# Adjacency and basis products of a four-layer graph network, issued per batch as 64x64x64 quarters of TensorE instead of 128x128x128 block-diagonal products

## The chip, the cores and the metric

The kernel runs on one core of a Trainium2 chip. The metric is the device time of one launch in microseconds (us); three executions of the kernel before took 2379.05, 2380.96 and 2382.34 us, so the median is 2380.96 us. The engines are named as in the profile: PE is TensorE's matmul stream and PEld its weight loads, DVE is VectorE, ACT is ScalarE, POOL is GpSimd and SP the queue of SyncE that issues DMAs.

## What is computed

The input x holds 128 batches of 64 nodes with 256 features, in float32, and one 64x64 adjacency matrix `adj` serves all batches. Four layers follow one another, and each ends in `x = layernorm(x + layer(x))`:

```python
# layer 0: two graph convolutions, then LSTMs over windows of 1 to 4 nodes
h = relu(einsum('ts,bsh->bth', adj, x @ Wg0 + bg0))
h = relu(einsum('ts,bsh->bth', adj, h @ Wg1 + bg1))
for p in 1..4: the last node of each window of p nodes becomes an LSTM's last state
# layer 1: normalized adjacency, two maps with batch norm over all rows
agg = einsum('nm,bmd->bnd', A_hat, x);  h = relu(bn(agg @ W1.T + b1));  out = bn(h @ W2.T + b2)
# layer 2: attention over 512 edges, 4 heads
# layer 3: U = eigenvectors of the normalized Laplacian (64x64)
agg = einsum('mn,bnd->bmd', U.T, x);  h = relu(agg @ W1 + b1)
out = einsum('nm,bmd->bnd', U, h @ W2 + b2)
```

So `adj` (layer 0, twice), `A_hat` (layer 1) and `U` (layer 3, twice) are each a 64x64 matrix that is applied to the 64 nodes of every batch separately. These are the products that the change touches.

## The kernel before

X stays in SBUF for the whole program as 64 tiles of 128 rows and 256 features; one tile holds two batches, batch b in rows 64b to 64b+63. A group of four tiles (index q) is the unit of work of all the stages below.

**The matrices.** `bda`, `bdah`, `bdu` and `bdut` are 128x128 tiles with the 64x64 matrix twice on the diagonal and zeros elsewhere (`bdu` and `bdut` reuse the tiles of `bda` and `bdah` later on, which is why the profile names them so). One product of a tile's 128-feature half with such a matrix handles two batches at once, and half of what it multiplies is zeros. The result comes out transposed, features in the rows, which is what the next map wants as its moving operand. Each float32 matmul leaves two records in the trace, so counts of records are twice the counts of calls.

**Layer 0.** `convolve(g, H)` does a group of 16 tiles in four q. For each q it forms `axT` (line 1566, copied by ACT on line 1568), multiplies by wg0 (line 1574, DVE line 1575), then by wg1 (line 1584, DVE line 1586) and applies the adjacency again (line 1592) with a relu copy by ACT into H (line 1594). It is a generator that yields after every PSUM evacuation, 8 times for each q. The first group runs alone, beside the sorting of the edges (`sort_edges`). The other three run inside `windows(...)`, the LSTM (lines 1624 and 1628, gates on ACT line 1630): `paced` spreads their steps evenly over the LSTM's matmuls of p = 3 and 4. The convolution has two PSUM buffers of its own (`pp`, `bufs=2`), the LSTM four (`pq`). A computation of the eigenvectors of 64x64 size runs beside the LSTM on DVE, in small pieces that `pump` issues (its matmuls are on line 148, 64 rows of the array each).

**Layer 1.** A first loop over 16 q multiplies by `bdah` (line 1787), copies with ACT to `at` (line 1789), multiplies by w1 (line 1793, sixteen records of four output blocks), takes statistics with DVE (line 1794), and copies the result away with ACT (line 1795). In the first eight q, transposes of layer 0's last group follow (line 1661). PSUM has seven buffers here. The inner part reads:

```python
for k in range(2):
    ps = pp.tile([P, 512], F32, tag="ps", name="ps")
    for j in range(4):
        te.matmul(ps[:, j * P : (j + 1) * P], X[:, q * 4 + j, k * P : (k + 1) * P], bdah, start=True, stop=True)
    s.copy(at[:, k, :], ps)
for c in range(4):
    ...
```

**Layer 2** is not changed, but its `mixed` (line 2125) already issues 64x64x64 matmuls: for one batch (64 rows) the four heads alternate between the two column halves of the array; the second batch follows, in another PSUM bank.

**Layer 3** is a software pipeline over q with four stages: `basis` (line 2211, copied by ACT line 2213; POOL then adds a constant to X, line 2215), `first_map` (line 2221, DVE line 2224), `back` (line 2229, ACT line 2231) and `second_map` (line 2239, whose sum and norm are `Norm.add` and `flush`, lines 1234 to 1253). A call of `blocks` runs stage k on q-k in the order 0, 1, 2, 3. The last part of layer 2 (`values`: line 2125, then 2146) is interleaved with it, two steps for each block. Six PSUM buffers serve both.

The order on each engine is fixed when the program is built: each engine works through its list in order, and a wait at the head of the list holds up all behind it.

Of the kernel before, what the change touches and what calls it, by code (L numbers as in the profile page):

```python
# [7 lines left out]
F32 = mybir.dt.float32  # L8
# [6 lines left out]
N = 64  # L15
NB = 128
D = 256
P = 128
# [1241 lines left out]
def tile_adj_resnorm(ctx: ExitStack, tc: tile.TileContext, I: dict, out: bass.AP, layers: int = 4):  # L1260
# [65 lines left out]
    bdah = const.tile([P, P], F32, tag="bdah", name="bdah")  # L1326
    bdu, bdut = bda, bdah


    ek = ctx.enter_context(tc.tile_pool(name="ek", bufs=1))  # L1330
    et = ctx.enter_context(tc.tile_pool(name="et", bufs=1))
# [178 lines left out]
    with tc.tile_pool(name="lw", bufs=1) as lw, tc.tile_pool(  # L1510
# [48 lines left out]
        def convolve(g, H):  # L1559

            for q in range(TG // 4):
                axT = lc.tile([P, 2, 512], F32, tag="ay", name="axT")
                for k in range(2):
                    ps = pp.tile([P, 512], F32, tag="ps", name="ps")
                    for j in range(4):
                        te.matmul(ps[:, j * P : (j + 1) * P], X[:, g * TG + q * 4 + j, k * P : (k + 1) * P],
                                  bda, start=True, stop=True)
                    s.copy(axT[:, k, :], ps)
                    yield
                h1 = lc.tile([P, 2, 512], F32, tag="h1", name="h1")  # L1570
                for c in range(2):
                    ps = pp.tile([P, 512], F32, tag="ps", name="ps")
                    for k in range(2):
                        te.matmul(ps, wg0[:, k, c * P : (c + 1) * P], axT[:, k, :], start=(k == 0), stop=(k == 1))
                    v.tensor_tensor(
                        h1[:, c, :].rearrange("p (b n) -> p b n", n=N), ps.rearrange("p (b n) -> p b n", n=N),
                        negc[:, c, None, :].to_broadcast([P, 8, N]), ALU.max)
                    yield
                y2 = lc.tile([P, 4, D], F32, tag="ay", name="y2")
                for j in range(0, 4, 2):  # L1580
                    ps = pp.tile([P, 512], F32, tag="ps", name="ps")
                    for i in range(2):
                        for k in range(2):
                            te.matmul(ps[:, i * D : (i + 1) * D], h1[:, k, (j + i) * P : (j + i + 1) * P],
                                      wg1[:, k, :], start=(k == 0), stop=(k == 1))
                    v.tensor_tensor(y2[:, j : j + 2, :], ps.rearrange("p (i d) -> p i d", i=2),
                                    b2c[:, None, :].to_broadcast([P, 2, D]), ALU.add)
                    yield
                for c in range(2):
                    ps = pp.tile([P, 512], F32, tag="ps", name="ps")  # L1590
                    for j in range(4):
                        te.matmul(ps[:, j * P : (j + 1) * P], y2[:, j, c * P : (c + 1) * P], bda,
                                  start=True, stop=True)
                    s.activation(H[:, c].rearrange("p (m j) -> p j m", j=TG)[:, q * 4 : q * 4 + 4, :],
                                 ps.rearrange("p (j m) -> p j m", j=4), AF.Relu)
                    yield

        def windows(l0, H, p, w, side):

# [78 lines left out]
        with tc.tile_pool(name="gk", bufs=1) as gk:  # L1678
            sort = sort_edges(gk, pq, "pq")
            next(sort)  # L1680
            for k, _ in enumerate(convolve(0, H)):
                if k == 3:
                    second_bias(gk)
                if k == 7:
                    degrees()
                if k > 9:
                    next(sort, None)
            load_x(1)
            for _ in sort:
                pass  # L1690
        LOAD = {p: (TG * 2 * (N // p) / 512) * (6 + 16 * (p - 1)) for p in range(1, 5)}
        with tc.tile_pool(name="l0g", bufs=1) as l0:
            back = iter(())
            for g in range(NT // TG):


                side = paced(back, TG // 2, LOAD[1] + LOAD[2] - 4)
                for p in (1, 2):
                    windows(l0, H, p, weights(p), side)
                for _ in back:  # L1700
                    pass
                last, more = H, iter(())
                if g < NT // TG - 1:
                    if g < NT // TG - 2:
                        load_x(g + 2)
                    H = new_h(g + 1)
                    more = convolve(g + 1, H)
                side = paced(more, TG * 2, LOAD[3] + LOAD[4] - 4)
                for p in (3, 4):
                    windows(l0, last, p, weights(p), side)  # L1710
                for _ in more:
                    pass
                if g < NT // TG - 1:
                    back = residual(g, last, pr, "pr")
# [66 lines left out]
    for q in range(NQ):  # L1781
        nc.sync.dma_start(xd[q], xq(q))
        at = la.tile([P, 2, 512], F32, tag="at", name="at")
        for k in range(2):
            ps = pp.tile([P, 512], F32, tag="ps", name="ps")
            for j in range(4):
                te.matmul(ps[:, j * P : (j + 1) * P], X[:, q * 4 + j, k * P : (k + 1) * P], bdah,
                          start=True, stop=True)
            s.copy(at[:, k, :], ps)  # L1789
        for c in range(4):  # L1790
            ps = pp.tile([P, 512], F32, tag="ps", name="ps")
            for k in range(2):
                te.matmul(ps, w1[:, k, c * P : (c + 1) * P], at[:, k, :], start=(k == 0), stop=(k == 1))  # L1793
            v.bn_stats(st1[:, c, q, :], ps)
            s.copy(first(q, c), ps)
        next(back, None)
        if q < NQ - 1:
            pump(4.5 if q < 8 else 6.5 if q < NQ - 2 else 3)
# [108 lines left out]
    with ExitStack() as l2:  # L1907
# [291 lines left out]
        with tc.tile_pool(name="l3s", bufs=2) as s3, tc.tile_pool(name="l3p", bufs=6, space=PSUM) as p3:  # L2199
# [5 lines left out]

            def basis(q):
                ag[q] = s3.tile([P, 2, 512], F32, tag="ag", name="ag")
                for k in range(2):
                    ps = bank()
                    for j in range(4):  # L2210
                        te.matmul(ps[:, j * P : (j + 1) * P], X[:, q * 4 + j, k * P : (k + 1) * P], bdu,  # L2211
                                  start=True, stop=True)
                    s.copy(ag[q][:, k, :], ps)
                for j in range(4):
                    nc.gpsimd.tensor_tensor(X[:, q * 4 + j, :], X[:, q * 4 + j, :], cb, ALU.add)

# [7 lines left out]
                v.tensor_tensor(h[q], four(ps), nb1[:, None, :].to_broadcast([P, 4, P]), ALU.max)  # L2224

            def back(q):
                ps, a = bank(), h.pop(q)
                for j in range(4):
                    te.matmul(ps[:, j * P : (j + 1) * P], a[:, j, :], bdut, start=True, stop=True)  # L2229
                uh[q] = s3.tile([P, 4, P], F32, tag="uh", name="uh")  # L2230
                s.copy(uh[q], four(ps))

            def second_map(q):
                a = uh.pop(q)
# [12 lines left out]
            def blocks():  # L2247

                NQ = NT // 4
                for q in range(NQ + 3):  # L2250
                    for k, stage in enumerate((basis, first_map, back, second_map)):
                        if 0 <= q - k < NQ:
                            stage(q - k)
                    yield
# [70 lines left out]
```

## Time and profile before

| what | value |
|---|---|
| executions | 2379.05, 2380.96, 2382.34 us |
| median | 2380.96 us |
| span of the profiled execution (first to last instruction) | 2376.5 us |
| median less that span | 4.5 us |
| PE busy / DVE / ACT / POOL | 96% / 76% / 41% / 4% |
| granted PE clock, mean | 0.992 |

The profile gives the span of the profiled execution and no separate launch time for it; the executions around it lie 2.6 to 5.8 us above the span, which is what stands before the first and after the last instruction. A busy PE in the page means that some matmul is in flight; how densely they are issued is read from their starts.

The stages, by the records: layer 0 lasts until 1508 us (its first convolution until 69 us), the first loop of layer 1 from 1508 to 1658 us, its second loop and the scores of layer 2 until about 2086 us, the values of layer 2 from 2086 us on, with layer 3 from 2190 us to the end.

### The profile page before, as it was taken

The numbers are of one execution on the slowest core, as the hardware profiler recorded it, in microseconds if no ns is written. First come the engines' busy times: TensorE is split into PE (matmuls) and PEld (weight loads), VectorE is DVE, ScalarE is ACT, GpSimd is POOL, SyncE is SP. The second block draws the span as 40 slices with busy tenths as digits, with TensorE's granted clock in tenths as the row PEclk, the third lists the DMA queues.
The fourth block names the chain that finished last, engine by engine and source line by source line (L and its number), as shares of the span: only waits on it lengthen the run. The fifth ranks groups of instructions, "written<-read, shape, count | busy, mean of one in ns | idle before, by whom it ended". The sixth has DMA issues, their size and how long they took to land. (4 is left out here: it accounts for less than half of the span.)

```text
span 2376.5 us, 29696 instructions
## 1 busy us (share of the span) xinstructions
PE 2285.6 (96%) x9094; PEld 1228.5 (52%) x9094; DVE 1807.6 (76%) x8366; ACT 973.5 (41%) x1754; POOL 88.0 (4%) x134
## 2 busy tenths in 40 slices
PE   8999999999999999999999999999999999999897
PEld 6445654444565544664544654454434343345787
DVE  5666666677887888878888888788867886656587
ACT  2432222242333243333243322333427875557575
POOL 0000000000000000000000000000000000101431
PEclk9999999999999999999999999999999999999999
DMA  7000000000100010100000110011210010311532
GB/s 221 22 17 36 1 36 1 36 18 18 54 1 36 1 54 18 54 2 35 23 32 18 54 36 1 1 69 71 87 56 23 27 39 27 102 36 43 135 96 72
DMA packets 44661, 101.52 MB, mean 43 GB/s; under 512 B 5296, under 2 KB 23856, under 8 KB 43216
## 3 DMA queue, kind: packets, MB, share of 16 engines
q1 hardware_dynamic: 38656, 84.90, 10.4%
q0 software_dynamic: 3984, 14.40, 2.2%
q8 instruction: 72, 1.18, 0.2%
q14 instruction: 93, 0.76, 0.1%
q10 hardware_dynamic: 1856, 0.28, 0.1%
HBM read 67.97 MB, written 31.59 MB: 42 GB/s over the span
## 5 line engine op out<-in xcount | busy, mean ns | idle before, releaser
L1624 PE MATMUL pq<-H,wi 128*128 128x512 f32 (+1 forms) x2016 | 836.1, 548 | 6.3 <-DVE H L1653 4.0
L1630 ACT ACTIVATE gate<-pq,bl 128x512 f32<-128x512 f32 (+1 forms) x504 | 317.5, 634 | 802.8 <-PE pq L1628 657.8
L1624 PEld LDWEIGHTS pq<-H,wi 128*128 128x128 f32 x2016 | 372.7, 191 | 332.2 <-issue 256.3
L1628 PE MATMUL pq<-lh,wh 128*128 128x512 f32 (+1 forms) x1152 | 483.6, 536 | 15.5 <-DVE lh L1648 12.3
L1628 PEld LDWEIGHTS pq<-lh,wh 128*128 128x128 f32 x1152 | 213.4, 190 | 212.0 <-issue 128.2
L2027 DVE SCALAR_TENSOR_TENSOR xs<-xs 128x512 f32<-128x512 f32 x256 | 166.0, 683 | 57.0 <-ACT xs L2026 56.0
L2026 ACT COPY xs<-l 128x512 f32<-128x512 f32 x256 | 136.6, 585 | 73.8 <-PE l L2019 40.5
L1646 ACT ACTIVATE gate<-lc 128x512 f32<-128x512 f32 (+1 forms) x144 | 83.5, 580 | 165.6 <-DVE lc L1642 80.2
L2019 PE MATMUL l<-edge_s,xq 64*128 64x512 f32 x512 | 134.0, 616 | 9.5 <-ACT xs L2026 4.8
L1982 PE MATMUL m<-wqv,xT 128*128 128x512 f32 (+1 forms) x264 | 121.0, 596 | 0.9 <-DVE xT L1972 0.8
L1793 PE MATMUL ps<-at,w 128*128 128x512 f32 x256 | 115.0, 600 | 3.9 <-ACT at L1789 3.4
L1843 PE MATMUL ps<-h,w 128*128 128x512 f32 x256 | 112.3, 596 | 2.4 <-ACT h L1837 2.4
L1253 ACT ACTIVATE X<-X,ln_sh,ln_rs 128x256 f32<-128x256 f32 x192 | 99.9, 591 | 31.5 <-DVE ln_sh L1249 22.9
L1237 DVE BATCH_NORM_STATS2 ln_st<-X 128x6 f32<-128x256 f32 x256 | 98.6, 416 | 2.4
L142 DVE COPY AQR<-eps 64x192 f32<-64x192 f32 (+1 forms) x125 | 35.0, 280 | 83.5 <-PE eps L148 83.5
L1982 PEld LDWEIGHTS m<-wqv,xT 128*128 128x128 f32 x264 | 46.7, 189 | 73.9 <-issue 55.0
L1644 DVE TENSOR_TENSOR gate<-gate 128x512 f32<-128x512 f32 (+1 forms) x72 | 43.5, 605 | 47.4 <-ACT gate L1630 46.6
L1843 PEld LDWEIGHTS ps<-h,w 128*128 128x128 f32 x256 | 47.9, 190 | 60.6 <-issue 50.7
L2019 PEld LDWEIGHTS l<-edge_s,xq 64*128 64x128 f32 x512 | 46.1, 186 | 60.5 <-issue 31.7
L1793 PEld LDWEIGHTS ps<-at,w 128*128 128x128 f32 x256 | 46.6, 190 | 58.7 <-issue 46.0
L1653 DVE TENSOR_TENSOR H<-gate 128x512 f32<-128x512 f32 (+1 forms) x72 | 46.8, 650 | 35.0 <-ACT gate L1646 29.7
L129 DVE SCALAR_TENSOR_TENSOR CS<-GA,qE 64x1 f32<-64x1 f32 x294 | 61.7, 210 | 9.7
(586 smaller groups left out, 3231.5 us busy)
## 6 DMA issues: line engine op xcount, KB each, us to landing
wi<-in_WihT_dram SPq DMA_DIRECT2D x16, 1024.0 KB, 4.8
wh<-in_WhhT_dram SPq DMA_DIRECT2D x12, 1024.0 KB, 6.8
xd<-X SPq DMA_DIRECT2D x16, 512.0 KB, 2.8
X<-xd SPq DMA_DIRECT2D x16, 512.0 KB, 3.4
xv<-xv SPq DMA_DIRECT2D x32, 256.0 KB, 2.0
xr<-xv POOLq DMA_DIRECT2D x32, 256.0 KB, 2.9
X<-in_x_dram SPq DMA_DIRECT2D x15, 512.0 KB, 8.9
out_dram<-X SPq DMA_DIRECT2D x15, 512.0 KB, 2.9
```

Of the source, the lines that this page charges most:

```text
L1237: nc.vector.bn_stats(st, self.X[:, k, :])
L1253: nc.scalar.activation(x, x, AF.Identity, bias=sh[:, k : k + 1], scale=rs[:, k : k + 1])
L1624: te.matmul(ps, wi[:, kk, o * P : (o + 1) * P], at(kk, k), start=(kk == 0), stop=(k == 0 and kk == 1))
L1628: te.matmul(ps, wh[:, kk, o * P : (o + 1) * P], hst[:, kk, :M], start=False, stop=(kk == 1))
L1630: s.activation(gates[gt][:, c, :M], ps, AF.Tanh if gt == 2 else AF.Sigmoid, bias=bl[:, p - 1, o : o + 1])
L1646: s.activation(g[2], cs, AF.Tanh)
L1793: te.matmul(ps, w1[:, k, c * P : (c + 1) * P], at[:, k, :], start=(k == 0), stop=(k == 1))
L1843: te.matmul(ys[c], w2[:, k, c * P : (c + 1) * P], h[:, k, :], start=(k == 2), stop=(k == 1))
L1982: te.matmul(pss[i][:, cols], xT[:, i, c, :], wqv[:, c, cols], start=(c == 0), stop=(c == 1))
L2019: mms.append(te.matmul(pl[i][:, b, :], xq[i][r, c * P : (c + 1) * P], GG[r, :], start=True, stop=True))
L2026: taken.append(s.copy(x, pl[i][:, b, :]))
L2027: ready.append(v.scalar_tensor_tensor(x, x, 0.2, x, ALU.mult, ALU.max))
```

## The change

A new helper `by_node` issues each product as four matmuls of 64 rows, 64 columns and 64 moving columns: two feature halves c (the column half of the array) by two batches b (the row half), batch b into PSUM bank b. It takes the place of the block-diagonal products in lines 1566, 1592, 1787, 2211 and 2229. Two banks are in use at a time, both are complete only when all the quarters are, and each evacuation copies one batch out of its bank into the interleaved columns of the same SBUF tile (`side_of`). Every copy still has 512 elements for each partition, except in `back`, where one copy of 512 becomes two of 256.

Around that, the convolution yields 6 times for each q instead of 8 (`paced` gets 24 steps in place of 32, and the steps of `sort_edges` in the first group are placed anew), and a block of layer 3 runs `back` directly after `basis`, before `first_map`.

```diff
+    def by_node(both, tiles, bd):
+        n = len(tiles)
+        for j, x in enumerate(tiles):
+            for k in range(x.free_size() // P):
+                for c in range(2):
+                    for b in range(2):
+                        r, o = slice(b * N, (b + 1) * N), (k * n + j) * N
+                        te.matmul(both[b][c * N : (c + 1) * N, o : o + N],
+                                  x[r, k * P + c * N : k * P + (c + 1) * N], bd[r, r], start=True, stop=True)
+    def side_of(a, b):
+        return a.rearrange("p (m b n) -> p b m n", b=2, n=N)[:, b]
...
-                for k in range(2):
-                    ps = pp.tile([P, 512], F32, tag="ps", name="ps")
-                    for j in range(4):
-                        te.matmul(ps[:, j * P : (j + 1) * P], X[:, g * TG + q * 4 + j, k * P : (k + 1) * P],
-                                  bda, start=True, stop=True)
-                    s.copy(axT[:, k, :], ps)
-                    yield
+                both = [pp.tile([P, 512], F32, tag="ps", name="ps") for _ in range(2)]
+                by_node(both, [X[:, g * TG + q * 4 + j, :] for j in range(4)], bda)
+                for b in range(2):
+                    s.copy(side_of(axT.rearrange("p k f -> p (k f)"), b), both[b])
+                yield
...
-                for c in range(2):
-                    ps = pp.tile([P, 512], F32, tag="ps", name="ps")
-                    for j in range(4):
-                        te.matmul(ps[:, j * P : (j + 1) * P], y2[:, j, c * P : (c + 1) * P], bda,
-                                  start=True, stop=True)
-                    s.activation(H[:, c].rearrange("p (m j) -> p j m", j=TG)[:, q * 4 : q * 4 + 4, :],
-                                 ps.rearrange("p (j m) -> p j m", j=4), AF.Relu)
-                    yield
+                both = [pp.tile([P, 512], F32, tag="ps", name="ps") for _ in range(2)]
+                by_node(both, [y2[:, j, :] for j in range(4)], bda)
+                for b in range(2):
+                    s.activation(
+                        H.rearrange("p c (b n j) -> p b c j n", b=2, j=TG)[:, b, :, q * 4 : q * 4 + 4, :],
+                        both[b].rearrange("p (c j n) -> p c j n", c=2, j=4), AF.Relu)
+                yield
...
-                if k == 3:
+                if k == 2:
                     second_bias(gk)
-                if k == 7:
+                if k == 5:
                     degrees()
-                if k > 9:
-                    next(sort, None)
+                if k > 6:
+                    for _ in range(1 + (k % 6 in (0, 5))):
+                        next(sort, None)
...
-                side = paced(more, TG * 2, LOAD[3] + LOAD[4] - 4)
+                side = paced(more, TG * 3 // 2, LOAD[3] + LOAD[4] - 4)
...
         at = la.tile([P, 2, 512], F32, tag="at", name="at")
-        for k in range(2):
-            ps = pp.tile([P, 512], F32, tag="ps", name="ps")
-            for j in range(4):
-                te.matmul(ps[:, j * P : (j + 1) * P], X[:, q * 4 + j, k * P : (k + 1) * P], bdah,
-                          start=True, stop=True)
-            s.copy(at[:, k, :], ps)
+        both = [pp.tile([P, 512], F32, tag="ps", name="ps") for _ in range(2)]
+        by_node(both, [X[:, q * 4 + j, :] for j in range(4)], bdah)
+        for b in range(2):
+            s.copy(side_of(at.rearrange("p k f -> p (k f)"), b), both[b])
...
             def basis(q):
                 ag[q] = s3.tile([P, 2, 512], F32, tag="ag", name="ag")
-                for k in range(2):
-                    ps = bank()
-                    for j in range(4):
-                        te.matmul(ps[:, j * P : (j + 1) * P], X[:, q * 4 + j, k * P : (k + 1) * P], bdu,
-                                  start=True, stop=True)
-                    s.copy(ag[q][:, k, :], ps)
+                both = [bank() for _ in range(2)]
+                by_node(both, [X[:, q * 4 + j, :] for j in range(4)], bdu)
+                for b in range(2):
+                    s.copy(side_of(ag[q].rearrange("p k f -> p (k f)"), b), both[b])
...
             def back(q):
-                ps, a = bank(), h.pop(q)
-                for j in range(4):
-                    te.matmul(ps[:, j * P : (j + 1) * P], a[:, j, :], bdut, start=True, stop=True)
+                both, a = [bank() for _ in range(2)], h.pop(q)
+                by_node(both, [a[:, j, :] for j in range(4)], bdut)
                 uh[q] = s3.tile([P, 4, P], F32, tag="uh", name="uh")
-                s.copy(uh[q], four(ps))
+                for b in range(2):
+                    s.copy(side_of(uh[q].rearrange("p j f -> p (j f)"), b), both[b][:, : 4 * N])
...
-                    for k, stage in enumerate((basis, first_map, back, second_map)):
+                    for k, stage in ((0, basis), (2, back), (1, first_map), (3, second_map)):
```

## The prediction

> **What bounds the kernel now.** I read the page's first parts, the groups of instructions, then the timeline around the products that are replaced, and last the table of stretches.
>
> ```profile
> PE 2285.6 (96%) x9094; PEld 1228.5 (52%) x9094; DVE 1807.6 (76%) x8366; ACT 973.5 (41%) x1754; POOL 88.0 (4%) x134
> ...
> L1566 PE MATMUL ps<-bda,X 128*128 128x128 f32 x256 | 36.7, 288 | 3.5 <-DVE rs L1546 2.9 <-ACT H L1594 0.5
> L1592 PE MATMUL ps<-bda,y 128*128 128x128 f32 x256 | 35.1, 278 | 1.3 <-DVE y L1586 1.2
> L2125 PE MATMUL m<-mc,xr 64*64 64x64 f32 x1024 | 34.1, 227 | 9.8 <-DMA xr<-xv 7.9 <-DVE xT L1972 0.8 <-ACT xv L1996 0.5
> L1787 PE MATMUL ps<-bdah,X 128*128 128x128 f32 x256 | 31.3, 275 | 0.0
> L2211 PE MATMUL ps<-bda,X 128*128 128x128 f32 x256 | 31.1, 275 | 0.0
> L2229 PE MATMUL ps<-bdah,h 128*128 128x128 f32 x128 | 17.2, 276 | 0.0
> ```
>
> PE is the bound nearly everywhere, and the five products hold 36.7 + 35.1 + 31.3 + 31.1 + 17.2 = 151 us of it in the union of their records (one ends 0.27 us after its start, so I cost them by starts). What they are worth per stage is read from the timeline. Layer 3 beside the values, on PE (start, time, group):
>
> ```profile
> 2250.75 0.97 PE L2125 MATMUL m<-mc,xr 64*64 64x64 f32 x32
> 2251.66 1.99 PE L2146 MATMUL ps<-wo,yT 128*128 128x256 f32 x8
> 2253.49 1.95 PE L2211 MATMUL ps<-bda,X 128*128 128x128 f32 x16
> 2255.27 1.95 PE L2221 MATMUL ps<-w,ag 128*128 128x128 f32 x16
> ```
>
> Sixteen records of a block-diagonal product take 2255.27 - 2253.49 = 1.78 us from start to next start, 111 ns each. The 32 quarter records of line 2125 take 0.91 us, 28 ns each, so four quarters cost 114 ns: a quarter in that order gains nothing. All depends on how many quarters run at a time. Layer 1, PE and then ACT:
>
> ```profile
> 1520.76 1.95 PE L1787 MATMUL ps<-bdah,X 128*128 128x128 f32 x16
> 1522.55 7.11 PE L1793 MATMUL ps<-at,w 128*128 128x512 f32 x16
> 1529.50 0.61 PE L1661 MATMUL ps<-ident,H 128*128 128x128 f32 x4
> 1529.94 1.95 PE L1787 MATMUL ps<-bdah,X 128*128 128x128 f32 x16
> ```
>
> ```profile
> 1521.25 0.59 ACT L1795 COPY X<-ps 128x512 f32<-128x512 f32 x1 [1.13 <-DVE st L1794]
> 1521.86 0.59 ACT L1789 COPY at<-ps 128x512 f32<-128x512 f32 x1
> 1522.75 0.58 ACT L1789 COPY at<-ps 128x512 f32<-128x512 f32 x1 [0.30 <-PE ps L1787]
> ```
>
> Here PE has no gap: the first half of `at` is copied while the second is multiplied, and the second copy runs under the first map's 0.43 us records. In layer 3's steady part PE is full as well (30.00 of 30.00 us), with PEld at 26.56, DVE at 24.28 and ACT at 23.38:
>
> ```profile
> 2260.00:2290.00 30.00, 30.00 (x345) 26.56 (x342) 24.28 (x88) 23.38 (x50) 8.84 (x14) 1.00 0.30 89
> ```
>
> **The price of a burst.** Single records of line 2125 at 2250.75 us: the passes on one quarter of the array start 107 ns (first to second) and then 58 ns apart, always two quarters (one batch's two column halves) within 7 ns. The second batch's first pass starts 294 ns after the first batch's, long before that one is through, and where they overlap four passes, on four quarters and two banks, start within 10 ns at 2251.15 and again 58 ns later. So four at a time cost no more than two, though this is seen for two rounds only. `by_node` cycles through all four quarters; I take four at a time. A burst of 32 calls is 16 passes on each quarter: 0.107 + 14 x 0.058 = 0.92 us to the last start. Entering the 64x64 form costs 0.09 us (line 1624 to 148 takes 522 ns where 1624 to 1624 takes 429), leaving it 148 ns to the next full matmul. Together 0.92 + 0.15 + 0.09 = 1.16 us against 1.78: 0.62 saved a burst, 64 bursts, and sixteen of half size in `back`.
>
> The Trainium skill, "TensorE: Matmul & The Clock Gate", section "Wait — 56ns, not 53.3ns?", speaks against this: start-to-start never falls below about 25 ns, however few columns move. By it a burst's 64 passes would take 1.60 us, and the sum below would come out some 42 us higher (an estimate from that page). The starts of 2 to 7 ns between quarters in this trace disagree, at least over short stretches.
>
> **Layer 0 beside the LSTM** (24 bursts). Before: 24 x 1.78 = 42.8 us. After: the passes alone are 24 x (0.92 + 0.06) = 23.5; in the built order PE changes between full and 64-row form 307 times instead of 254 (the eigenvector pieces of line 148 sit in some bursts and share the switch), 53 x 0.09 = 4.9; bursts cut in pieces restart some 20 times at 0.05, 1.0. Gain 13.4 us. Against it: ACT takes both copies in a row, 2 x 1.04 us for H and 2 x 0.58 for `axT`, where a yield lay between. The gates of line 1630 queue behind them, then the LSTM's next state; their four PSUM buffers cover about 2 us. I take off 2 us (bounds 0 and 10). The steps lie about 7 us of LSTM matmuls apart, which hides the wait for the pair of banks: net -11.4, between -13.4 and -3.
>
> **The first convolution** (8 bursts, no LSTM beside it). Here the copies are bare. Before, the first map starts at 25.73, right behind the product at 23.84 to 25.5. After, both banks end together; ACT copies for 2 x 0.58; then the map starts. The same between the second adjacency product and the next q: two H copies of 1.04 us must end before both banks are free, where PE waited 0.26 us. Followed from q to q this adds 1.4 us for each of two q; in the other two the matmuls of the edge sort (lines 1443, 1472) now stand in these gaps and give most of it back. The first q gains a wait of about 0.9 us, since a degree matmul stands ahead of the map. Net +2, between -2 and +7.
>
> **Layer 1** (16 bursts). The built order puts nothing between the burst and the maps. From the burst's first start, 0.09 us later than before: last pass 0.92, its end 0.22 and the signal 0.04 later, copies 1.18 to 1.77 and 1.77 to 2.36, first map 2.41, so 2.50 on the old scale against 1.79 (q below 8). From q = 8 ACT is held by line 1795 until 1.43: 2.76 against 2.06. That is 0.7 later, less 0.1 us of a stall at the second record that goes. So the 0.62 is not only lost: each q gets 0.6 us longer. 15 x 0.6 = +9 (the first q waits for ACT either way), I take +9.5; bounds +6 (ACT free sooner) and +13.
>
> **Layer 3.** `basis` and `back` adjoin and share the switch: 24 passes on each quarter, 0.107 + 22 x 0.058 + 0.24 = 1.63 us against 1.78 + 0.89 = 2.67. Saved 1.04 a block; each copy has a block's time before it is needed. ACT gets 2 x 0.37 instead of 0.57, +0.17. In the eight steady blocks of 11.86 us DVE works 9.6 and waits for ACT 0.8, ACT works 9.4: 10.8 is feasible, and I take 0.85 of the 1.04: -6.8. The first four blocks run into the wait for `xr` at 2224.67 to 2232.47, behind the attention scatter and POOL's additions; the built order puts four additions, not eight, between the fetch and that load, and the scatter ahead of three: -2.5. In the last blocks DVE works 5.75 of 6.2 us: -1.2. Net -10.5, between -16 and -5.
>
> **Sum.** -11.4 + 2 + 9.5 - 10.5 = -10.4: the span 2376.5 becomes 2366.1; with the 4.5 us between it and the median, 2370.6.
>
> **Rivals.** (1) Two quarters at a time, as line 2125 shows for most of its length. Then each burst has 16 more rounds of 0.058 = 0.93 us. Beside the LSTM 24 x 0.93 = 22 worse than above, the first convolution 7.5, layer 1 15, layer 3 (PE again the bound) 16: 61 more, 2431. For it: 28 ns is the only rate sustained. Against: the two rounds of four, and line 1958, where four column strips with 512 columns start within 20 ns. It decides early: at rounds of 68 ns instead of 58 the gain is gone. (2) The exposed copies cost more: ACT's doubled bursts stall the LSTM at every step, the upper bounds of layer 0 (-3, +7) and layer 1 (+13) with -8 in layer 3: +9, 2390; for it, PE's largest LSTM wait is already for DVE's h behind the gates (12.3 us in 15 waits). (3) Everything hides: -13.4 - 2 + 6 - 16 = -25, 2355; against it, layer 1's order leaves nothing to hide behind. (4) The terms cancel within 0.2%, about what a measurement of this kernel can tell from no change (2376.2 to 2385.7): layer 3 held by DVE at -5 and the LSTM by ACT at -6 suffice. That the change does not do what it says is excluded by the built order, which has the quarters in every place.
>
> **How the numbers follow.** Forecast 2360 to 2376: 0.47. Rival 3, 0.09. Rival 4, 0.16. Rival 2 beyond that, 0.08. Rival 1 and rounds in between, 0.20. Faster: 0.47 + 0.09 = 0.56; same 0.16; slower 0.28. The range reaches from rival 3 to the middle of the way to rival 1: 2356 to 2402; its own range for the forecast is 2360 to 2376.
>
> **What would show it.** In the changed profile a burst of 64 records of the new line should last about 0.98 us; 1.8 us is rival 1. PE's switches show as 0.09 and 0.15 us. In layer 1 the period of a q should grow from 9.18 to about 9.8 us, with PE waiting about 1.4 us for `at`; if it shrinks, that step is wrong. In layer 3 the steady block should take about 11.0 us instead of 11.86. Layer 0 should end about 9 us earlier, near 1499; if it ends later although bursts last 0.98 us, the copies on ACT are the cause, and waits of the gates or of line 1628 should have grown.

## The result, and the profile after

The changed kernel takes 2402.24 us (median of 4 runs, 2400.45 to 2403.98) against 2380.01 us for the kernel before, measured beside it: a ratio of 1.0096, 95% interval 1.0083 to 1.0109. It is slower by about 1%, where I forecast 0.4% faster. The profiled execution has a span of 2400.3 us, 23.8 more than before.

Cut into stages (from the start to the first LSTM matmul; from there to the first product of layer 1; from there to the second loop of layer 1; the rest), the two executions compare as follows, in us, each number rounded by itself:

| | first convolution | LSTM part | layer 1, first loop | rest, with layer 3 | span |
|---|---|---|---|---|---|
| before | 69.0 | 1439.4 | 155.2 | 712.9 | 2376.5 |
| after | 83.3 | 1439.6 | 173.2 | 704.1 | 2400.3 |
| difference | +14.3 | +0.2 | +18.0 | -8.8 | +23.8 |
| predicted | +2 | -11.4 | +9.5 | -10.5 | -10.4 |

The page of the changed kernel, engines and the group of layer 1's maps:

```profile
PE 2267.8 (94%) x12550; PEld 1181.6 (49%) x12550; DVE 1812.3 (76%) x8366; ACT 966.8 (40%) x1769; POOL 88.3 (4%) x134
...
L1804 PE MATMUL ps<-at,w 128*128 128x512 f32 x256 | 119.5, 620 | 25.9 <-ACT at L1800 25.9
```

PE works 18 us less, and the maps alone stand 25.9 us behind the copy to `at`. Before, the waits for that copy in layer 1's first loop were, in total, times and longest:

```profile
PE ps L1793 <- ACT at L1789: 3.4, 3, 3.0
```

Layer 1 of the changed kernel on PE, two blocks, and then the copy on ACT (start, time, group, and in brackets the idle time before it and what ended it):

```profile
1528.29 8.77 PE L1804 MATMUL ps<-at,w 128*128 128x512 f32 x16 [4.21 <-ACT at L1800]
1536.90 0.60 PE L1673 MATMUL ps<-ident,H 128*128 128x128 f32 x4
1537.43 1.16 PE L1337 MATMUL ps<-bdah,X 64*64 64x64 f32 x64
1539.77 7.13 PE L1804 MATMUL ps<-at,w 128*128 128x512 f32 x16 [1.18 <-ACT at L1800]
```

```profile
1538.64 1.07 ACT L1800 COPY at<-ps 128x512 f32<-128x512 f32 x2 [0.23 <-PE ps L1337]
```

The 64 records of a burst last 0.94 us from first to last start (1.16 us as a union of their records), as priced. But PE then has nothing to do until both copies are through: 1539.77 - 1537.43 = 2.34 us from the burst to the first map, where the product before took 1.79. And the maps of the first block take 8.77 us, not 7.13. (Their wait of 4.21 us is not new in full: before, the first block waited 3.0 us.) The table of stretches of the changed kernel says why; its column PEclk is the granted clock (1.00 is full):

```profile
26.40:29.80 3.40, 2.10 (x90) 1.82 (x89) 0.00 (x0) 1.88 (x2) 0.00 (x0) 0.99 1.01 403
29.80:36.60 6.80, 5.59 (x38) 2.82 (x31) 0.90 (x2) 1.07 (x2) 0.00 (x0) 0.50 1.09 354
60.50:63.90 3.40, 2.44 (x63) 2.21 (x59) 2.93 (x6) 1.79 (x2) 0.00 (x0) 1.00 0.02 5
63.90:74.10 10.20, 10.20 (x81) 5.56 (x81) 2.86 (x9) 3.13 (x5) 0.00 (x0) 0.50 0.00 0
1524.00:1528.20 4.20, 0.07 (x7) 0.00 (x0) 2.28 (x4) 1.82 (x4) 0.00 (x0) 1.00 0.06 6
1528.20:1531.60 3.40, 3.31 (x4) 1.51 (x5) 0.00 (x0) 0.04 (x1) 0.00 (x0) 0.50 0.00 0
1620.40:1623.80 3.40, 1.45 (x4) 0.73 (x5) 2.97 (x16) 1.56 (x3) 0.00 (x0) 1.00 0.03 5
1623.80:1627.20 3.40, 3.40 (x6) 1.34 (x5) 0.91 (x2) 0.59 (x1) 0.00 (x0) 0.50 0.00 0
```

In these rows, after a stretch in which PE was busy for 0 to 2.44 of 3.40 us, the clock is at half for 3.4 to 10.2 us, and the maps that run in it are longer: 8.77 us instead of 7.13 with 3.4 us at half clock. The first convolution has 20.5 us at half clock after its start-up (before: none), layer 1's first loop 10.2 us (before: none). "None" holds for this one profile of the kernel before: l3_only below, whose first convolution and layer 1 are the code of before, has 3.4 us at half clock in the one and 6.8 us in the other, and takes 70.3 and 158.1 us for them instead of 69.0 and 155.2.

Layer 3's steady part is as forecast, PE full and a block of 10.93 us instead of 11.86:

```profile
2294.18 1.99 PE L2157 MATMUL ps<-wo,yT 128*128 128x256 f32 x8
2296.11 1.16 PE L1337 MATMUL ps<-bda,X 64*64 64x64 f32 x64
2297.09 0.65 PE L1337 MATMUL ps<-bdah,h 64*64 64x64 f32 x32
2297.67 2.05 PE L2230 MATMUL ps<-w,ag 128*128 128x128 f32 x16
```

Both products of a block take 2297.67 - 2296.11 = 1.56 us, where I had 1.63 against 2.67.

### The profile page after: what moved, and what is told of

It reads as the page before. It is cut to its first block, busy times and chain, and to the rows that moved or that the text cites. A ratio compares the mean times of both kernels' runs of the same rounds, so it can differ in the third digit from the quotient of the medians.

```text
span 2400.3 us, 36629 instructions
## 1 busy us (share of the span) xinstructions
PE 2267.8 (94%) x12550; PEld 1181.6 (49%) x12550; DVE 1812.3 (76%) x8366; ACT 966.8 (40%) x1769; POOL 88.3 (4%) x134
## 3 DMA queue, kind: packets, MB, share of 16 engines
q1 hardware_dynamic: 38656, 84.90, 10.4%
## 5 line engine op out<-in xcount | busy, mean ns | idle before, releaser
L2037 ACT COPY xs<-l 128x512 f32<-128x512 f32 x256 | 136.7, 586 | 73.7 <-PE l L2030 40.5
L1804 PE MATMUL ps<-at,w 128*128 128x512 f32 x256 | 119.5, 620 | 25.9 <-ACT at L1800 25.9
L2030 PEld LDWEIGHTS l<-edge_s,xq 64*128 64x128 f32 x512 | 46.1, 186 | 60.6 <-issue 31.7
L1665 DVE TENSOR_TENSOR H<-gate 128x512 f32<-128x512 f32 (+1 forms) x72 | 46.8, 650 | 34.4 <-ACT gate L1658 29.1
L1805 DVE BATCH_NORM_STATS2 st<-ps 128x6 f32<-128x512 f32 x64 | 44.2, 691 | 36.3 <-PE ps L1804 36.3
```

The source lines that it names most:

```text
L2030: mms.append(te.matmul(pl[i][:, b, :], xq[i][r, c * P : (c + 1) * P], GG[r, :], start=True, stop=True))
L2037: taken.append(s.copy(x, pl[i][:, b, :]))
```

## The experiments

The theory after this reading: a burst is as cheap as priced. The loss comes from where its copies stand bare, that is, where PE has nothing else to do until they are through (first convolution, layer 1), by the wait itself and by the clock that falls in the waits. Beside the LSTM the saving is made and then lost to new waits. Layer 3 gains. The rivals are in the expectations.

**Undoing one part.** Layer 1's first loop back to the full-width product (l1_old), that and the first convolution back (both_old), and layer 3 alone changed (l3_only):

```diff
-        both = [pp.tile([P, 512], F32, tag="ps", name="ps") for _ in range(2)]
-        by_node(both, [X[:, q * 4 + j, :] for j in range(4)], bdah)
-        for b in range(2):
-            s.copy(side_of(at.rearrange("p k f -> p (k f)"), b), both[b])
+        for k in range(2):
+            ps = pp.tile([P, 512], F32, tag="ps", name="ps")
+            for j in range(4):
+                te.matmul(ps[:, j * P : (j + 1) * P], X[:, q * 4 + j, k * P : (k + 1) * P], bdah,
+                          start=True, stop=True)
+            s.copy(at[:, k, :], ps)
```

In both_old the first convolution has, besides, for both of its products with `bda`:

```diff
+                if g == 0:
+                    for k in range(2):
+                        ps = pp.tile([P, 512], F32, tag="ps", name="ps")
+                        for j in range(4):
+                            te.matmul(ps[:, j * P : (j + 1) * P], X[:, g * TG + q * 4 + j, k * P : (k + 1) * P],
+                                      bda, start=True, stop=True)
+                        s.copy(axT[:, k, :], ps)
+                        yield
+                else:
...
```

and the old numbers in the loop that paces the degrees and the sort.

> The changed kernel with layer 1's first loop put back to full products with one copy per half; everything else as changed. Theory (copies of both batches bare on the matrix engine's queue, plus half clock behind those waits): the loop, 173.2 us from its first product to the second loop in the changed kernel, falls back to about 155, so about 2402 - 18 = 2384 us, with no half-clock interval between 1528 and 1655 us. Rival A (only the copies, the clock dips come from elsewhere, and stay): about 2402 - 13 = 2389. Rival B (the loss of this loop is caused by what layer 0 leaves over, for instance late eigenvector pieces): the loop stays above 165, 2395 or more.

> The changed kernel with layer 1's first loop and the first convolution (the one without LSTM beside it, and the pacing of the edge sort and degrees there) put back to the full-width products; the 64x64 form is left in the 24 products beside the LSTM and in layer 3. Theory: 2402 - 18 - 14 = 2370 us, faster than the kernel before by about 9 us, all of it from layer 3 (LSTM stretch 1439 us as in both). Rival (the 14 us of the first convolution return later, since the eigenvector pieces behind its end set the pace of group 0): about 2380.

> The kernel before with the change in layer 3 alone. Theory: -8.8 us, about 2371, and equal to the kernel with the 64x64 form beside the LSTM too within 2 us, since the LSTM stretch takes 1439.4 and 1439.6 us in the two kernels. Rival (the LSTM stretch does gain some 5 us from the 64x64 form, and loses it again to what the first convolution left late): then this one is 5 us slower than the one with the form beside the LSTM.

Measured: l1_old 2384.65 us (ratio to before 1.0023, 1.0012 to 1.0035), both_old 2373.08 (0.997, 0.9958 to 0.9983), l3_only 2372.66 (0.9974, 0.9962 to 0.9986). Layer 1's loop took 155.2 us in l1_old, without a half-clock stretch, so that part of the change costs 17.6 us, and the first convolution (68.5 us in both_old) another 11.6. The LSTM part with the 64x64 form (both_old) and without it (l3_only) makes no difference, 0.4 us in the medians: LSTM part and layer 1's loop together take 1594.8 and 1594.3 us. What the change gains is layer 3's, 6.2 us (both_old) to 6.6 us (l3_only) by the medians. All three came within about 3 us of what was expected. The last column of the table above flatters the change: the same layer 3 took 704.1 us with the rest of the program there, and 705.7 to 713.2 us in the ten other profiles that have it and keep the eigenvector pieces in place.

**Hiding the copies.** The bursts of block q+1 ahead of the maps of block q (l1_pipe), the rest as changed:

```diff
+    ahead = aggregate(0)
     for q in range(NQ):
-        nc.sync.dma_start(xd[q], xq(q))
-        ...
+        at = ahead
+        if q < NQ - 1:
+            ahead = aggregate(q + 1)
```

Here `aggregate(q)` holds the store to `xd`, the burst and the two copies, unchanged.

> The changed kernel with layer 1's first loop software-pipelined: the 64x64 products of block q+1 are issued ahead of the maps of block q, so that the copies have a block's maps (7 us) to hide behind. Theory (bare copies and the clock that falls in the gaps): the period per block falls from 9.9 (first eight) and 9.5 us to about 8.6 and 8.4, that is 16 x 0.5 below the full-width product's 9.2 and 9.0: the loop from 173 to about 147, 2376 us in all. Rival A (ScalarE or VectorE is the bound of this loop, six copies, four bn_stats and the norm a block): the loop goes no lower than the 155 of the full-width product, about 2384. Rival B (a 64x64 burst costs more than its records show): above 160, 2389 or more.

Measured 2375.88 us (0.9987, 0.9975 to 0.9998), 26.4 us below the changed kernel. The loop took 143.6 us, 11.6 less than with the full-width product, with a period of 8.60 us in the first eight blocks. (That the total is just the expected 2376 is in part luck: the loop is 3.4 us shorter than expected, and what follows it 5.7 us longer than in the profile of the changed kernel. The second loop of layer 1 gives 1.7 us back: 115.7 instead of 114.0 us in every kernel with the pipelined first loop.) PE in this kernel:

```profile
1552.55 1.16 PE L1337 MATMUL ps<-bdah,X 64*64 64x64 f32 x64
1553.64 7.13 PE L1811 MATMUL ps<-at,w 128*128 128x512 f32 x16
1560.61 0.61 PE L1673 MATMUL ps<-ident,H 128*128 128x128 f32 x4
1561.15 1.16 PE L1337 MATMUL ps<-bdah,X 64*64 64x64 f32 x64
```

The burst costs 1553.64 - 1552.55 = 1.09 us to the next full matmul, and no idle time stands in front of the maps. So in layer 1 the burst was never the trouble; the order around it was.

**The clock by itself.** Matmuls whose results are thrown away, in the waits of the first convolution and of layer 1 (fill):

```diff
             ps = pp.tile([P, 512], F32, tag="ps", name="ps")
+            if c == 0:
+                for n in (512, 256):
+                    tc.keep_in_program_order(te.matmul(ps[:, :n], bdah, w1[:, 0, :n], start=True, stop=True))
             for k in range(2):
                 te.matmul(ps, w1[:, k, c * P : (c + 1) * P], at[:, k, :], start=(k == 0), stop=(k == 1))
```

In the first convolution `fill` writes to a bank of the LSTM's gates, with (512, 256) columns behind the first product and (512, 512, 256) behind the second:

```diff
+        def fill(g, *n):
+            if g == 0:
+                ps = pq.tile([P, 512], F32, tag="pq", name="pq")
+                for m in n:
+                    tc.keep_in_program_order(
+                        te.matmul(ps[:, :m], ones, wg0.rearrange("p k f -> p (k f)")[:, :m], start=True, stop=True))
```

> The changed kernel with matmuls whose results are thrown away standing in the waits for the copies: 512 and 256 columns (1.29 us at full clock) behind each first product of the first convolution and each product of layer 1, 512, 512 and 256 columns (2.15 us) behind each second product of the first convolution. Theory (gaps on the matrix engine drop the granted clock to 0.5 and the maps behind run at half speed): no half-clock interval between 20 and 75 us nor between 1520 and 1690; the first convolution falls from 83 to about 75 us, layer 1's loop from 173.2 to about 168, 2389 us in all. Rival A (the copies alone, the clock does not matter): no gain in either, a few us of loss, 2402 to 2410. Rival B (the clock falls for another reason than the gaps): the same dips stay.

Measured 2397.22 us (1.0064, 1.0045 to 1.0082). The total is 8 us above the expected 2389. The first convolution took 78.4 us and layer 1's loop 168.8, the latter as expected, the former 3 us more; the stages behind them took 711.3 us instead of 704.1, so that the profile's span is only 3.7 us shorter than the changed kernel's. The stretches of both in this kernel:

```profile
8.00:78.40 70.40, 66.90 (x690) 42.11 (x686) 41.23 (x120) 15.48 (x21) 0.00 (x0) 1.00 0.57 186
...
1516.50:1685.30 168.80, 160.17 (x1391) 80.92 (x1390) 125.41 (x499) 58.41 (x105) 1.16 (x2) 1.00 0.13 50
```

The granted clock is full throughout by this column, and useless work makes both stages shorter (by 4.9 and 4.4 us). 2.3 of the 4.9 us come from the first map, ahead of the stretches listed above: it takes 3.6 us here and 5.9 in the changed kernel, from the same start at 14.8. So by these two profiles the clock is a cause of its own, of some 9 of the 32 us (the fillers cost some time themselves, and one profile of a stage can differ from the next by some 3 us, as l3_only shows). The rest remains without it: 9.4 and 13.6 us above before.

**Grouping or form.** Full-width products in layers 0 and 1, but both banks filled first and then both copied, with the pacing of the change (pair_all):

```diff
-                by_node(both, [X[:, g * TG + q * 4 + j, :] for j in range(4)], bda)
-                for b in range(2):
-                    s.copy(side_of(axT.rearrange("p k f -> p (k f)"), b), both[b])
+                for k in range(2):
+                    for j in range(4):
+                        te.matmul(both[k][:, j * P : (j + 1) * P], X[:, g * TG + q * 4 + j, k * P : (k + 1) * P],
+                                  bda, start=True, stop=True)
+                for k in range(2):
+                    s.copy(axT[:, k, :], both[k])
```

> The changed kernel with full-width products everywhere in layer 0 and layer 1 but the changed grouping kept: both PSUM banks are filled first, then both are copied, in one step. It separates the grouping from the 64x64 form. Theory: the grouping bares the copies, so the first convolution stays long (about 83 + 8 x 0.6 = 88 us, against 69 with one copy per bank) and layer 1's loop takes 173 + 16 x 0.6 = 183 us. Beside the LSTM: if the switches of form ate the 64x64 gain there, the stretch is 1439 us as in both kernels; if the grouping ate it (both copies in a row on ScalarE, waits for h), it is about 1439 + 24 x 0.6 = 1453 us. Rival for the first convolution (the degree matmul ahead of the first map and the pacing of the sort are the cause, not the copies): 75 us or less.

Measured 2372.73 us (0.997, 0.996 to 0.998), as fast as layer 3's change alone; the expectation failed in both stages. The first convolution took 70.7 us, in the range of the rival, and layer 1's loop 158.2, of which 6.8 us at half clock from 1512.0, as in l3_only; the LSTM part took 1437.2. Layer 1's wait for the copies in this kernel:

```profile
PE ps L1812 <- ACT at L1808: 3.5, 3, 3.0
```

I had reasoned that both copies would come bare. They don't: here a bank holds one half of the features of both batches, so the first bank is complete after half the product, its copy runs beside the other half, and the first map needs only that copy. `by_node` puts one batch into each bank, both banks end with the burst, and the first map needs both copies. So the grouping and the pacing of the edge sort cost next to nothing by themselves, which takes the pacing out of the rival. What is left is that both banks end together; this comes with the 64x64 form as `by_node` has it, and no kernel had that form with another split of the banks. In the first convolution the other half of the rival stays: in this order the degree matmul no longer stands ahead of the first map, where the changed kernel waits 3.9 us for it.

**Beside the LSTM.** The 24 bursts there issued twice (lstm_double):

```diff
-                by_node(both, [X[:, g * TG + q * 4 + j, :] for j in range(4)], bda)
+                for _ in range(2 if g else 1):
+                    by_node(both, [X[:, g * TG + q * 4 + j, :] for j in range(4)], bda)
```

> The changed kernel with each of the 24 products beside the LSTM (groups 0 to 2) issued twice into the same banks, 0.94 us more of the matrix engine's time each, 7.5 us a group; switches and copies as changed. If the matrix engine sets the pace there: phases p=3 and p=4 of each group get 7.5 us longer, 22.6 in all (1439.6 to 1462). If VectorE or the eigenvector chain sets it, the growth is under half of that; my theory has group 0 paced by VectorE (under 4 us) and groups 1 and 2 by the matrix engine (6 us or more each).

Measured 2426.85 us in a single run. The phases p=3 and p=4 of groups 0, 1 and 2 grew by 9.5, 8.5 and 6.8 us, 24.8 in all (the whole LSTM part by 20.9, since the last group, which has no bursts in these phases, took 4.4 us less). PE sets the pace in every group; that VectorE paces group 0 was wrong. The saved time should then have come, unless something grew with it. The same matmuls without the eigenvector pieces around them, in the 64x64 form (nop_after) and with full-width products (nop_pair):

```diff
-                                pump((0.8 * 6 / 4 if k == 0 else 1.6 * 8 / 6) * M / 512 * PACE * (0.85 if p < 3 else 1.1))
+                                pump((0.8 * 6 / 4 if k == 0 else 1.6 * 8 / 6) * M / 512 * PACE * (0.85 if p < 3 else 0.0))
```

> The changed kernel with no eigenvector pieces issued in the LSTM phases p=3 and p=4, the ones that hold the products; the pieces then run after the LSTM, so only those phases are read, not the total. To be compared with the next run, which has full-width products in the same grouping and no pieces either. Theory (the 64x64 form saves 20 us of matmul time beside the LSTM and loses it to waits that the eigenvector steps and the LSTM's state take in the new order, and to switches): without the pieces the six phases of groups 0 to 2 are 8 to 14 us shorter than with full-width products (they are 1.9 us shorter with the pieces: 710.2 against 712.9 and within 3 us of it). Rival (the burst itself costs more than its records show, whatever is around it): 0 to 4 us.

> The changed grouping with full-width products in layers 0 and 1, and no eigenvector pieces in the LSTM phases p=3 and p=4; the partner of the run before. Theory: these phases are 8 to 14 us longer than there. Rival: 0 to 4 us.

(With the pieces the difference is 712.9 - 710.2 = 2.7 us; the 1.9 in the text is a slip.) Measured: 220.4 against 222.4 us in each of the three groups, so 6.0 us together, between the theory and the rival. A group's eight products take 14.21 us full-width and 7.86 in the 64x64 form. Of these 6.35 us, 12 changes of form (four bursts are cut in two by LSTM matmuls) take back 12 x (0.093 + 0.148) = 2.9. New waits appear, for which nop_pair has no line at all:

```profile
PE pq L1636 <- DVE H L1665: 0.6, 2, 0.4
PE pq L1640 <- DVE lh L1660: 0.3, 2, 0.2
```

This fits a longer product that had covered the LSTM's own chain of gates, state and next matmul. With the eigenvector pieces the waits are larger. The waits of PE over the whole LSTM part, in the changed kernel (in total, times, longest):

```profile
PE pq L1640 <- DVE lh L1660: 15.2, 17, 2.8
PE eps L148 <- DVE Hh L129: 13.0, 29, 1.4
PE pq L1636 <- DVE H L1665: 5.4, 6, 4.0
```

Before, these are 12.3, 9.2 and 4.0 us. The longest of the second line stands inside a burst (timeline of the changed kernel, PE):

```profile
424.79 0.61 PE L1337 MATMUL ps<-bda,X 64*64 64x64 f32 x25
426.77 0.24 PE L148 MATMUL eps<-Hh,AQR 64*64 64x64 f32 x1 [1.36 <-DVE Hh L129]
```

An eigenvector step has been placed in the middle of the burst, its input is still on its way through VectorE, and the rest of the burst and the LSTM's matmuls queue behind it. In lstm_double the same three waits are nearly unchanged (14.5, 13.8, 5.4 us) with 23 us more matmuls, so more time for VectorE does not shrink them; that they follow from the order is the reading that fits. Why the order puts the step there I only argue: a burst is 32 instructions where the product was 8, and the built order may take it for longer than it is. That was not tried.

**Combinations.** The first convolution full-width and layer 1 pipelined, LSTM and layer 3 in the 64x64 form (g0old_l1pipe); all of layer 0 as before, layer 1 pipelined and layer 3 in the 64x64 form (convold_l1pipe); and the same with full-width products in the pipelined layer 1 (full_l1pipe). The edits are those shown above.

> First convolution with full-width products as before, 64x64 form beside the LSTM, pipelined layer 1, 64x64 form in layer 3. Theory (the terms of the stages add): the kernel with both the first convolution and layer 1 put back (2373.1 us) less the 11.6 us that the pipelined loop is shorter than the full-width one (155.2 to 143.6 us): about 2361.5, faster than the kernel before by 0.7%. Rival (layer 1's end waits for eigenvector pieces that then come later, and gives the gain back in the second loop): 2368 or more.

> The kernel before with two changes: layer 3 in the 64x64 form, and layer 1's first loop in the 64x64 form with the products of block q+1 issued ahead of the maps of block q. All of layer 0 as before. Theory: the kernel with layer 3 alone changed (2372.7 us) less 155.2 - 143.6 = 11.6 us: 2361. Rival (eigenvector pieces that had cover in the longer loop come due in the second loop): 2366 or more.

> The same with full-width products in layer 1's first loop, in the same pipelined order: a control for what of the loop's 11.6 us comes from the order and what from the 64x64 form. Theory (the full-width product was already hidden well, matrix-engine waits of 3.9 us in the loop in all): the loop 151 to 154 us, so 2370, and the 64x64 form itself is worth 16 x 0.6 = 9 us once its copies are hidden. Rival (the order alone brings it): the loop 146 or less.

Measured: 2368.43 us (0.9948, 0.9934 to 0.9961), 2359.33 (0.993, 0.9916 to 0.9943) and 2361.97 (0.9934, 0.992 to 0.9947). The second is the fastest version of this study, 18.9 us below before by the medians, as expected from adding the terms. The first missed its 2361.5; it came to the rival's 2368. In its profile the first convolution took 73.7 us, where the same code took 68.5 us in both_old, and what follows layer 1's first loop 713.2 instead of 708.3. Of these 4.9 us the second loop, which the rival named, has 1.7, with 3.4 us of half clock at its start (1657.3); 3.3 stand between the start of layer 2's values and layer 3, with 6.8 us of half clock (2083.9). The first convolution has a stretch at half clock that both_old lacks:

```profile
53.00:56.40 3.40, 3.40 (x28) 2.94 (x28) 2.04 (x8) 0.81 (x2) 0.00 (x0) 1.00 0.03 5
56.40:66.60 10.20, 10.20 (x12) 3.18 (x11) 2.31 (x5) 2.27 (x3) 0.00 (x0) 0.50 0.00 0
```

Here PE waited for nothing in the 3.4 us ahead: the records cover all of them, though 14 of the 28 are the edge sort's products with a single moving column. l3_only has the same for 3.4 us from 56.5. So in the first convolution the clock also falls without a bared copy, and what makes it fall in one run and not in the next is open. The control came near the rival: the loop took 149.9 us full-width and 143.6 in the 64x64 form, so the order alone brings 5.3 of the 11.6 us and the form 6.3, not 9. In the totals these two kernels can't be told apart.

## Why the prediction was wrong

The total missed by 34 us: the first convolution by 12.3, the LSTM part by 11.6, layer 1 by 8.5 and layer 3 by 1.7. Two steps failed. Where the copies stand bare, the term was too small: the regular wait was as forecast, but the sum had no half clock, no longer waits in single blocks, and 0.9 us for the degree matmul. Beside the LSTM, the allowance of 2 us for waits was too small, and its cause was the wrong one.

- **The price of a burst was right.** 0.92 us to the last start against 0.94 measured, four quarters at a time; entering the form costs 0.093 us and leaving it 0.148 us, as taken. Rival 1 is out. The Trainium skill's floor of about 25 ns from start to start ("TensorE: Matmul & The Clock Gate", section "Wait — 56ns, not 53.3ns?") would have meant 1.60 us; 64 starts in 0.94 us are 15 ns each, so it does not hold between quarters of the array.
- **First convolution: the step that failed most against its bounds** (+2, bounds -2 to +7; measured +14.3 in the profile, 11.6 by the medians). The sum had all behind the copies at full clock; the profile has 20.5 us at half clock, which can cost half of that. The wait for the degree matmul ahead of the first map was 3.9 us, not 0.9, and the map started 2.5 us later than before (14.81 against 12.36). The two waits for the copies of H are there as forecast (1.1 us each, at 28.3 and 45.0). Fillers remove 4.9 us; 9.4 remain. That the waits for the copies brought the half clock is shown for none of its three stretches by itself: the last, 10.2 us from 63.9, also stands behind the edge sort's one-column products, as the ones in l3_only and g0old_l1pipe do.
- **Layer 1: right mechanism, half its size** (+9.5, bounds to +13; measured +18.0). The undisturbed blocks take 9.90 us instead of 9.20, just the forecast 0.7, and 9.52 instead of some 9.03 from q = 8. Added to that are 10.2 us at half clock, worth 4.4 us by the fillers, which the sum does not contain, 1.2 us more of wait in the first block (4.2 against 3.0), and waits of 2.3 to 2.7 us in three others, instead of 1.2 to 1.3: in two of them ACT has work for the norm (`is_s`, line 1214) ahead of the copies, in the third a copy that had waited for VectorE's statistics.
- **LSTM part: the allowance for waits** (-11.4; measured +0.2). A burst's 0.94 us to the last start instead of 1.78 makes 20 us less for the 24 (forecast 42.8 - 23.5 = 19.3). PE changes form 307 times instead of 254, as forecast. But PE's waits in this part grew from 31.7 to 41.2 us, by 9.5, and the time at half clock from 13.7 to 20.5 us, which can cost 3.4, where I had allowed 2 (bounds 0 to 10). The other 7 us or so, which I did not measure one by one, are left for the changes of form and slower starts (forecast 4.9 + 1.0). The cause given, ACT's doubled copies, is not what grew: pair_all issues the same two copies in a row and has 31.6 us of waits. Those that grew are for VectorE's eigenvector step and for the LSTM's state. The bound of -3 missed it as well.
- **Layer 3 was right where it is steady** (six periods of 11.85 us became 10.93, and one of 10.75 became 9.83: -6.4 against -6.8 forecast) **and at its end** (-1.25 against -1.2). The -2.5 of the first blocks does not repeat: from the first to the sixth map group it took 60.8 us before, 57.3 in the changed kernel, but 61.7 in l3_only. In the eleven profiles with this layer 3 that keep the eigenvector pieces in place this start took 57.3 to 64.7 us, and the changed kernel's own is the shortest, by luck. The whole is worth 6.2 to 6.6 us by the medians, within the bounds.

Rival 2 came nearest, with the right places in the first convolution and layer 1 (the copies exposed); the stall of the LSTM by ACT's copies that it also named is not what the profiles show, and no clock is in its price. The prediction's sign for it came half true: layer 0 ended 14.5 us later although bursts last as forecast, but all except 0.2 us of that is the first convolution's. What none of the four had is that a wait on PE can cost more than its length, because the clock may fall with it: some 9 of the 32 us. That the other 23 are waits, slower starts and the order is what remains when the clock is full; it was not split further.

## What to carry to other kernels

Before an accumulation is split over two PSUM banks, ask when each bank is complete and which of them the next matmul needs: a product 0.6 us shorter lost 1%, most of it because both banks ended together and their copies stood bare. Give such a product a stage of independent matmuls behind it (one block of software pipelining turned +18 us in that loop into -11.6), and price repeated waits of 1 to 4 us on PE with the half clock that may follow. Where the order of instructions is built around a product, a shorter product also takes away cover; count what stood behind it.

## What the runs showed of the hardware

In five of six places the granted clock fell without PE standing idle for a whole 3.4 us. In the changed kernel the stretches of half clock start on a raster of 3.41 us (29.8, 46.8, 63.9, 1528.2, 1623.8 and 1654.5 us lie whole multiples of it apart, within 0.1 us), and the 3.4 us ahead of a start held between 0.0 (at 1528.2) and 2.44 us of PE work. The Trainium skill ("TensorE: Matmul & The Clock Gate", section "What's actually happening") has a free-running window of 3413 ns, which agrees, and half rate after an idle window, which fits 1528.2 alone: windows with PE busy for 60 to 72% sufficed in the first convolution, all three with a 64x64 burst in them, and in g0old_l1pipe and l3_only one that the records cover in full. I can't give a threshold, since other windows with as little work kept the full clock.

Bursts can also stall with no releaser on record. In l3_only the first block of layer 3 reads (PE):

```profile
2206.95 0.28 PE L1337 MATMUL ps<-bdah,h 64*64 64x64 f32 x2 [0.27 <-issue]
2207.70 0.36 PE L1337 MATMUL ps<-bdah,h 64*64 64x64 f32 x6 [0.47 <-issue]
```

Nothing that the profile shows released these records ("issue"); they are six such waits with 2.3 us in all (2.4 to 3.1 us in both_old, l1_old and fill), and in the changed kernel the same bursts ran without one. What held PE there stays open. It may be one reason why the gain of layer 3's first blocks did not repeat; half clock for 6.8 us from 2196.7 and 3.4 us from 2210.3 in the same blocks of l3_only is another.
